# Ordering pieces of work behind gathers, opening sums by their first product, and loading weights later, in a four-layer graph network

## The chip, the cores and the metric

The kernel runs on one core of a Trainium2 chip. Its engines run side by side, each through its own queue in order: TensorE (PE, matmuls, with its weight loads shown as PEld), VectorE (DVE), ScalarE (ACT), GpSimd (POOL), and SyncE (SP), which here only issues DMAs. The metric is the device time of one execution in microseconds (us); lower is better.

## The reference, cut to what matters

There are 16 batches of 1024 nodes with 128 features, each with its own 1024 x 1024 adjacency. Four layers follow each other, and each adds its result to `x`:

```python
h = relu(layernorm(x)); x = x + layer0(h, adj, W0, b0)   # neighbours' mean, two weights
h = relu(layernorm(x)); x = x + layer1(h, adj, W1, b1)   # neighbours' mean, one weight
h = relu(layernorm(x)); x = x + layer2(h, adj, ...)      # two rounds of messages, below
h = relu(layernorm(x)); x = x + layer3(h, adj, W, a)     # attention over neighbours

# layer2, for l in (0, 1):
a, b = x @ We1[l, :D], x @ We1[l, D:]
scores = sigmoid(relu(a[:, :, None] + b[:, None] + be1[l]) @ We2[l] + be2[l])
messages = (adj * scores) @ x
x = layernorm(x + relu([x, messages] @ Wu1[l] + bu1[l]) @ Wu2[l] + bu2[l]) * gamma[l] + beta[l]

# layer3
e = leaky(Wh1 + Wh2.T) * (adj + I), masked; softmax; @ Wh; elu
```

About 1.6% of the adjacency is not zero, and layer 2 needs scores only there.

## The kernel before

Layer 2 is done edge by edge. The adjacency is cut into 128 x 128 blocks, called buckets; up to four buckets form one of nine `GROUPS`. For every bucket `build` makes four 0/1 matrices (`on`, `onT`, `om`, `omT`) that choose the two end nodes of each edge. A piece `pn` (PE, L829, in the helper `turned`) transposes `on`, and ACT evicts it to `onT` (L869). A piece `pq` (PE, L873) follows, and DVE makes `omT` of it (L876). A piece `pm` (L829 again) transposes that, and ACT evicts it to `om` (L884). The three pieces share the one PSUM bank "a".

A `round` (two for each batch) walks over the nine groups. For each bucket `gather` (L1015) multiplies the `part` tiles by `on` and `om`, four matmuls into a bank `pre`; ACT and DVE evict it into the two halves of `hid` (L1031, L1032). `dots` (L1048) multiplies `hid` into `sc`; `ends` (L1069) makes `srow`; `scores` transposes it (`pt`) and multiplies it onto `onT` and `omT` (`val`, L1106); `scatter` (L1131) makes blocks of scores in a bank `p`; DVE multiplies them by the adjacency (`upd`, L1139); and `messages` (L1148) adds their products with `xf` to the sums `msg`, one bank for each half of the nodes (`acc0`, `acc1`). Layer 3 sums its products (L507) in banks `hp`, over three stretches of nodes. Before such a sum begins, `zero` (L562, L563) writes zeros into the whole bank with a matmul of a zero matrix, and all products of the sum then add to it (`start=False`).

Each normalization runs through `spread`: `bn_stats` on DVE (L231), small DVE operations (L234 to L239), a power on POOL (L242), and then either DVE's L249 and eight ACT operations (L251) in `normal`, or the DVE operations from L363 on and four subtracts (L365) with `gamma` and `beta` (L370, L371) in `update`. The transposes that follow a norm are at L259 (`tp`); those of the updated nodes at L1181; the adjacency's at L754 (`tn`).

Three lanes are woven together by `weave`: `main` (the rounds of batch b), `last` (the second update and layer 3 of batch b - 1) and `first` (layers 0 and 1, the last norm and the buckets of batch b + 1). Each lane yields a price; `weave` always continues the lane whose sum of prices, divided by the lane's length (`MAIN_US` 184, `LAST_US` 70, `FIRST_US` 115), is least. From the program so written a scheduler sets each engine's final order. `tc.issue_after(ins)` keeps what is written inside it behind the instruction `ins` in an engine's order. Batch 0's `first` lane runs alone at the start (`run`), after the weights' DMAs, which are issued on ACT's queue (L103 to L138); between its first yield and the rest stands `scaled` (L607), which rescales weights through a chain of small PE, DVE and ACT steps.

Of the kernel before, what the change touches and what calls it, by code (L numbers as in the profile page):

```python
# [9 lines left out]
F32 = mybir.dt.float32  # L10
F16 = mybir.dt.float16
FP8 = mybir.dt.float8e4
I32 = mybir.dt.int32
AF = mybir.ActivationFunctionType
# [26 lines left out]


MAIN_US = 184.0
FIRST_US = 115.0
LAST_US = 70.0


# [4 lines left out]
def tile_four_gnn_layers(  # L52
# [22 lines left out]
    nc = tc.nc  # L75
    B, N, D = x.shape
    P = 128
    T = N // P
    HALF = 512
    NH = N // HALF  # L80
# [32 lines left out]
    for l in range(L):  # L113
        nc.scalar.dma_start(we1_sb[:, l], we1[l].rearrange("(h d) e -> d h e", h=2))
    b1_bc = const.tile([P, D], F32, name="b1_bc")
    nc.scalar.dma_start(b1_bc, b1[None, :].broadcast_to([P, D]))
    be2_bc = const.tile([P, L], F32, name="be2_bc")
    nc.scalar.dma_start(be2_bc, be2.rearrange("l o -> o l").broadcast_to([P, L]))
    wu1_sb = const.tile([P, L, 2, KB * P], F32, name="wu1_sb")
    wu2_sb = const.tile([P, L, KB, D], F32, name="wu2_sb")  # L120
    for l in range(L):
        nc.scalar.dma_start(wu1_sb[:, l], wu1[l].rearrange("(h d) k -> d h k", h=2))
        nc.scalar.dma_start(wu2_sb[:, l], wu2[l].rearrange("(k p) d -> p k d", p=P))
    bu1_sb = const.tile([P, L, KB], F32, name="bu1_sb")
    bu2_sb = const.tile([P, L], F32, name="bu2_sb")
    with nc.allow_non_contiguous_dma(reason="small columns of weights, once"):
        nc.scalar.dma_start(bu2_sb, bu2.rearrange("l d -> d l"))
        for l in range(L):
            nc.scalar.dma_start(bu1_sb[:, l], bu1[l].rearrange("(k p) -> p k", p=P))
    rows = {}  # L130
    for name, v in (("gamma", gamma), ("beta", beta)):
        rows[name] = const.tile([P, L, D], F32, name=f"{name}_bc")
        for l in range(L):
            nc.scalar.dma_start(rows[name][:, l], v[l : l + 1, :].broadcast_to([P, D]))
    w3_sb = const.tile([P, D], F32, name="w3_sb")
    nc.scalar.dma_start(w3_sb, w3)
    a3_sb = const.tile([P, 2], F32, name="a3_sb")
    nc.scalar.dma_start(a3_sb, a3.rearrange("(h d) o -> d (h o)", h=2))  # L138

    half_neg = const.tile([P, T], F32, name="half_neg")  # L140
    nc.vector.memset(half_neg, -0.5)
# [42 lines left out]

    def over_t(v, n=T):
        return v[:, None, :].to_broadcast([P, n, D])

    class Layers:

# [273 lines left out]
    class Lane(Layers):  # L463
# [2 lines left out]

        fine = None

        def layer3(self, xt, strip, zero, name):

            yield from self.pre_ln(xt, f"3_{name}")
            wh = self.wide(f"wh_{name}")
            nc.vector.memset(wh[:, :, D : D + 1], 1.0)
            for sl, ps in self.by_node(self.hT, w3_sb, f"wh_{name}"):
                nc.scalar.activation(wh[:, sl, :D], ps, AF.Copy)
                yield 1
            wh2, wh1 = self.score_terms(self.hT, 1, name)
            yield 2  # L480

            o = self.scratch(f"o3_{name}")
            rsum = self.small([P, 2, T], "rsum", f"rsum_{name}")
            for lo, hi in L3_ROWS:
                n = hi - lo
                sums = self.one(f"hp_{name}_{lo}")[:, : n * (D + 1)]
                zero(sums)
                sums = sums.rearrange("p (t d) -> p t d", d=D + 1)
                for k in range(0, T, 2):
                    at = strip(k, lo, hi)  # L490
                    e = flat(self.scratch(f"e_{name}_{lo}_{k}"))[:, : 2 * n * P]
                    e = e.rearrange("p (k n) -> p k n", k=2)
                    for i in range(2):
                        if lo <= k + i < hi:
                            own = at[:, i, (k + i - lo) * P : (k + i + 1 - lo) * P]
                            nc.vector.tensor_add(own, own, ident)
                        nc.vector.scalar_tensor_tensor(
                            e[:, i], wh1[:, lo * P : hi * P], wh2[:, k + i : k + i + 1], at[:, i],
                            op0=OP.add, op1=OP.mult,
                        )  # L500
                    nc.vector.scalar_tensor_tensor(e, e, L3_ALPHA, e, op0=OP.mult, op1=OP.max)
                    nc.scalar.activation(e, e, AF.Exp)
                    nc.vector.scalar_tensor_tensor(e, at, 0.0, e, op0=OP.is_gt, op1=OP.mult)  # L503
                    yield 0.4 * n
                    for i in range(2):
                        for t in range(n):
                            nc.tensor.matmul(  # L507
                                sums[:, t], e[:, i, t * P : (t + 1) * P], wh[:, k + i, : D + 1],
                                start=False, stop=True, skip_group_check=True,
                            )  # L510
                        yield 0.4 * n
                nc.vector.tensor_copy(rsum[:, 0, lo:hi], sums[:, :, D])
                nc.vector.reciprocal(rsum[:, 1, lo:hi], rsum[:, 0, lo:hi])
                for t in range(n):
                    nc.scalar.activation(
                        o[:, lo + t], sums[:, t, :D], AF.Copy, scale=rsum[:, 1, lo + t : lo + t + 1]
                    )
            self.sums_seen(rsum, name)
            self.layer3_end(xt, o, name)
# [10 lines left out]
    class Edges:  # L530
        def __init__(self, stack):
# [16 lines left out]
                Lane(self.work, "m", N_SCRATCH["m"], self.psum, [(f"acc{h}", 1)]) for h in range(NH)  # L548
            ]
            self.own, self.rows_of, self.n_rows = own, {}, 0  # L550
            self.constants()

        def bank(self, tag, name):
# [1 line left out]

        def acc(self, h, name):

            ps = self.psum.tile([P, HALF], F32, tag=f"acc{h}", name=name)
            self.zero(ps)
            return ps  # L560

        def zero(self, ps):  # L562
            nc.tensor.matmul(ps, self.zero16, self.iota2[:, : ps.shape[1]], start=True, stop=True)  # L563

        def constants(self):
            con = self.con
            self.eye16 = con.tile([P, P], F16, name="eye16")
            nc.vector.tensor_copy(self.eye16, ident)
            self.zero16 = con.tile([P, P], F16, name="zero16")
            nc.vector.memset(self.zero16, 0.0)  # L570
            self.ones16 = con.tile([P, 1], F16, name="ones16")
            nc.vector.memset(self.ones16, 1.0)
            self.iota2 = con.tile([P, HALF], F16, name="iota2")
# [154 lines left out]
        def first(self, b):  # L728
# [44 lines left out]
                xt, lambda t: self.load("a", self.columns(s.adjT, t), f"l1_{b}_{t}"), rdeg, name  # L773
            )
            s.xf = self.work.tile([P, T, D], F32, tag="xf0", name=f"xf0_{b}", bufs=1)
            yield from lane.pre_ln(xt, f"2_{name}", dst=s.xf)
            s.xT = self.kept(lane.hT, "xT", f"xT0_{b}")
            s.x = self.kept(xt, "x", f"xk_{b}")
            yield from self.build(s, has, name)

# [44 lines left out]
        def turned(self, hot, ck, name):  # L825

            ps = self.a.one(name)
            for k in range(ck):
                nc.tensor.matmul(  # L829
                    ps[:, k * P : (k + 1) * P], hot[:, k * P : (k + 1) * P], self.eye16,  # L830
                    start=True, stop=True,
                )
            return ps

        def build(self, s, has, name):

# [4 lines left out]
            for g, grp in enumerate(GROUPS):  # L841
# [13 lines left out]
                for i, (t, u) in enumerate(grp):  # L855
# [13 lines left out]
                    nc.scalar.activation(onT, pn[:, : ck * P], AF.Copy, saturate=False)  # L869
                    yield 0.35  # L870
                    pq = self.a.one(f"pq_{nm}").rearrange("p (k m) -> p k m", m=P)
                    for k in range(ck):
                        nc.tensor.matmul(  # L873
                            pq[:, k], on[:, k * P : (k + 1) * P], rank[:, i], start=True, stop=True
                        )
                    nc.vector.tensor_tensor(  # L876
                        omT.rearrange("p (k m) -> p k m", m=P), pq[:, :ck],
                        self.odd[t == u][:, :, None].to_broadcast([P, ck, P]),
# [84 lines left out]
        class Group:  # L963
# [41 lines left out]
            def gather(self, i):  # L1005
# [4 lines left out]
                for d in range(self.nd):  # L1010
                    pre = path.m.one(f"pre_{self.name}_{i}_{d}")

                    for v, node, hot in ((d, t, on), (1 - d, u, om)):
                        for k in range(2):
                            nc.tensor.matmul(  # L1015
                                pre[:, :c], path.parts[node // Q][:, k, node % Q, v], hot[:, :c],
                                start=(hot is on and k == 0),
                                stop=(hot is om and k == 1),
                            )
                    if not self.diag:  # L1020
                        hid = path.work.tile(
                            [P, 2, C_OFF], F16, tag="hid", name=f"hid_{self.name}_{i}_{d}", bufs=N_HID
# [122 lines left out]
            def messages(self, d, upd):  # L1145
                def message(mb, up, lo, hi):
                    h = lo // Q
                    nc.tensor.matmul(  # L1148
                        self.msg[h][:, (lo - h * Q) * P : (hi - h * Q) * P],
                        self.xf[mb // Q][:, mb % Q], up,  # L1150
                        start=False, stop=True, skip_group_check=True,
                    )

                if d:
# [63 lines left out]
        def last(self, s, b):  # L1218
# [19 lines left out]
                yield from lane.update(L - 1, s.xf[h], xT, msgT, dst, f"{b}_{L - 1}_{h}")  # L1238
            xt = self.back(self.work.tile([P, T, D], F32, tag="x", name=f"xb_{b}"), s.x)
            nc.vector.tensor_add(xt, xt, new)  # L1240
            yield from lane.layer3(xt, strip, self.zero, f"{b}")
            nc.sync.dma_start(out[b].rearrange("(t p) d -> p t d", p=P), xt)

        def run(self):
# [2 lines left out]
            self.alone(self.a, "amcam")  # L1247
            first = self.first(0)
            next(first)
            self.scaled()  # L1250
            for us in first:
                if us is None:
                    break

            self.alone(self.a, "")
            self.a.banks = [self.own["c"], self.own["a"]]
# [197 lines left out]
```

## Time and profile before

| | |
|---|---|
| median of 3 runs | 5316.95 us (5308.2 to 5318.65) |
| profiled execution | 5325.15 us, span 5323.4 us |
| mean granted TensorE clock | 0.983 |
| PE, DVE, ACT, POOL busy | 93%, 79%, 57%, 4% |
| start, before the first gather | 0 to 134.7 us |
| a batch, in the middle | some 322 to 325 us |
| DMA, mean over the span | 104 GB/s |

A busy share is the part of the span in which the engine had an instruction under way. Matmuls overlap, so the time of one in the profile is longer than the distance from its start to that of the next. "a <- b" with a wait means that instruction a had nothing ahead of it on its engine and waited until b had ended. The granted clock is the share of full speed that TensorE's throttle allowed. The three runs shown are not the profiled execution, which took 8.2 us more than their median.

### The profile page before, as it was taken

What the parts mean: (1) busy time and instruction counts of PE and PEld (TensorE: products, weight loads), DVE (VectorE), ACT (ScalarE), POOL (GpSimd) and SP (SyncE); (2) the same over time, 40 slices, a digit from 0 to 9 for tenths busy, and PEclk for the clock granted to TensorE, in tenths of its full rate; (3) what the DMA queues carried; (4) which work ended last, traced back from release to release, by engine and by line L of the source; (5) the groups of instructions that cost most, each with busy time, mean ns of one, the idle gap of its engine ahead of it and who ended that gap; (6) DMA issues with size and microseconds to landing.
All of it is one profiled execution on the core that took longest, in us unless ns stands there. A gap on an engine that the chain in (4) does not pass through costs nothing.

```text
span 5323.4 us, 112270 instructions
## 1 busy us (share of the span) xinstructions
PE 4977.0 (93%) x45109; PEld 3739.4 (70%) x45109; DVE 4216.4 (79%) x9543; ACT 3044.9 (57%) x6790; POOL 189.3 (4%) x137
## 2 busy tenths in 40 slices
PE   6999999999999999999999999999999999999986
PEld 5766777777777777777777777777767777777664
DVE  4776787877879778797887978878797887978876
ACT  5556564655646556475564756656465564755543
POOL 0000000000000000000000000000000000000000
PEclk8999999999999999999999999999999999999998
DMA  6242425243252433424334242432524334243121
GB/s 185 64 143 88 123 62 150 83 127 108 75 147 74 134 94 89 141 73 125 96 107 130 62 138 88 121 115 72 154 71 136 97 89 142 74 126 93 57 63 48
DMA packets 740130, 554.47 MB, mean 104 GB/s; under 512 B 32273, under 2 KB 686353, under 8 KB 739601
## 3 DMA queue, kind: packets, MB, share of 16 engines
q1 hardware_dynamic: 734496, 545.58, 34.4%
q8 instruction: 356, 5.83, 0.5%
q10 hardware_dynamic: 5104, 1.65, 0.1%
q14 instruction: 174, 1.42, 0.1%
HBM read 446.44 MB, written 100.66 MB: 103 GB/s over the span
## 4 chain that ended last, share of the span: by engine, by line
PE 55%; DVE 22%; ACT 12%; DMA 5%; issue 3%; POOL 2%; SPq 0%; ACTq 0%; POOLq 0%; DVEq 0%
PE pre L1015 14%; PE p L1131 7%; DVE val L1106 7%; PE nb L289 6%; PE msg L1148 5%; PE bb L297 3%; PE sc L1048 3%; DVE hid L1032 3%; DMA at<-in_adj_dram 3%; PE h L343 3%; PE hp L507 3%; ACT hid L1031 2%; PE pq L873 2%; PE pn L829 2%; DMA a<-adjT 2%
## 5 line engine op out<-in xcount | busy, mean ns | idle before, releaser
L1031 ACT ACTIVATE hid<-pre 128x320 f16<-128x320 f32 (+1 forms) x2048 | 915.6, 455 | 666.8 <-PE pre L1015 603.0
L1032 DVE SCALAR_TENSOR_TENSOR hid<-pre,hid 128x320 f16<-128x320 f32 (+1 forms) x2048 | 1006.8, 505 | 240.6 <-ACT hid L1031 227.0
L1015 PEld LDWEIGHTS <-part 128*128 128x128 f16 x8192 | 746.0, 98 | 404.8 <-issue 196.6
L1015 PE MATMUL pre<-on,part 128*128 128x320 fp8e4 (+1 forms) x4096 | 985.2, 310 | 42.7 <-DVE hid L1032 32.5
L1015 PE MATMUL pre<-om,part 128*128 128x320 fp8e4 (+1 forms) x4096 | 962.9, 309 | 0.0
L1148 PE MATMUL msg<-upd,xf 128*128 128x128 f32 (+3 forms) x3008 | 595.3, 320 | 0.3 <-DVE upd L1139 0.3
L1106 DVE TENSOR_TENSOR val<-onT,u 128x768 f32<-128x768 fp8e4 (+1 forms) x576 | 561.1, 1010 | 3.1
L1131 PE MATMUL p<-val,omT 128*128 128x128 f16 x6528 | 507.3, 219 | 23.4 <-DVE val L1106 13.4
L1131 PEld LDWEIGHTS <-omT 128*128 128x128 fp8e4 x6528 | 423.0, 96 | 89.6 <-issue 62.3
L884 ACT ACTIVATE om<-pm 128x320 fp8e4<-128x320 f32 (+1 forms) x576 | 269.8, 468 | 292.0 <-PE pm L829 289.3
L1148 PEld LDWEIGHTS msg<-upd,xf 128*128 128x128 f32 x3008 | 410.3, 192 | 15.7 <-DVE upd L1139 1.6
L1106 DVE TENSOR_TENSOR val<-omT,u 128x768 f32<-128x768 fp8e4 x448 | 410.7, 950 | 0.0
L1139 DVE SCALAR_TENSOR_TENSOR upd<-p,adj 128x512 f32<-128x512 f32 x512 | 348.9, 681 | 74.9 <-PE p L1131 69.8
L1131 PE MATMUL p<-val,onT 128*128 128x128 f16 x4480 | 375.2, 219 | 2.4 <-DVE upd L1139 2.4
L869 ACT ACTIVATE onT<-pn 128x384 fp8e4<-128x384 f32 (+1 forms) x576 | 297.9, 517 | 120.9 <-PE pn L829 97.3
L507 PE MATMUL hp<-wh,e 128*128 128x129 f32 x2048 | 330.0, 283 | 14.3 <-DVE e L503 14.0
L1069 ACT ACTIVATE srow<-sc,be_s,down 128x128 f32<-128x128 f32 (+2 forms) x512 | 256.2, 541 | 142.6 <-PE sc L1048 140.2
L1131 PEld LDWEIGHTS <-onT 128*128 128x128 fp8e4 x4480 | 304.9, 97 | 46.7 <-issue 14.5
L507 PEld LDWEIGHTS hp<-wh,e 128*128 128x128 f32 x2048 | 282.5, 193 | 48.3 <-issue 19.7
L820 DVE TENSOR_SCALAR on<-far,wid 128x384 fp8e4<-128x384 f16 (+1 forms) x576 | 242.3, 427 | 67.2 <-PE pre L1015 59.5
L1048 PE MATMUL sc<-hid,slide 128*32 128x320 f16 (+1 forms) x4096 | 281.0, 317 | 14.6 <-DVE hid L1032 10.7
L816 ACT ACTIVATE far<-iota_off,mid 128x384 f16<-128x384 f16 x448 | 273.6, 629 | 7.8 <-DVE on L820 4.8
(217 smaller groups left out, 8118.5 us busy)
## 6 DMA issues: line engine op xcount, KB each, us to landing
at<-in_adj_dram SPq DMA_DIRECT2D x128, 512.0 KB, 3.9
ct<-in_adj_dram SPq DMA_DIRECT2D x128, 512.0 KB, 4.4
adjT<-tn SPq DMA_DIRECT2D x128, 512.0 KB, 5.2
l<-adjT SPq DMA_DIRECT2D x128, 512.0 KB, 4.3
adj<-adjT SPq DMA_DIRECT2D x256, 256.0 KB, 3.6
a<-adjT SPq DMA_DIRECT2D x128, 384.0 KB, 3.3
adj<-adjT SPq DMA_DIRECT2D x448, 64.0 KB, 2.3
adj<-adjT SPq DMA_DIRECT2D x192, 128.0 KB, 2.7
```

What stands on the lines that cost most here:

```text
L289: nc.tensor.matmul(ps, mat[:, k], z[:, k], start=(k == 0), stop=(k == T - 1))
L507: nc.tensor.matmul(sums[:, t], e[:, i, t * P : (t + 1) * P], wh[:, k + i, : D + 1], start=False, stop=True, skip_group_check=True,)
L816: nc.scalar.activation(far[:, : ck * P], self.iota[t == u][:, : ck * P], AF.Abs, bias=s.mid[:, i : i + 1])
L869: nc.scalar.activation(onT, pn[:, : ck * P], AF.Copy, saturate=False)
L1015: nc.tensor.matmul(pre[:, :c], path.parts[node // Q][:, k, node % Q, v], hot[:, :c], start=(hot is on and k == 0), stop=(hot is om and k = ...
L1031: nc.scalar.activation(hid[:, 0, :c], pre[:, :c], AF.Relu)
L1032: nc.vector.scalar_tensor_tensor(hid[:, 1, :c], pre[:, :c], 0.0, hid[:, 0, :c], op0=OP.max, op1=OP.subtract)
L1048: ins = nc.tensor.matmul(self.sc[g * G : (g + 1) * G, : self.c], self.path.slide[:, self.l, G - 1 - r : 2 * G - 1 - r], self.hid[self.done ...
L1106: nc.vector.tensor_tensor(pair[:, :, :ck], right, v.rearrange("p k i o -> p i k o").to_broadcast([P, 2, ck, P]), op=OP.mult,)
L1131: nc.tensor.matmul(self.ps[d][:, i], left[:, k], halves[:, k, :, h], start=(k, h) == terms[0], stop=(k, h) == terms[-1],)
L1139: nc.vector.scalar_tensor_tensor(upd, self.ps[d], S_SCALE, self.adj[:, d * Q : (d + 1) * Q], op0=OP.add, op1=OP.mult,)
L1148: nc.tensor.matmul(self.msg[h][:, (lo - h * Q) * P : (hi - h * Q) * P], self.xf[mb // Q][:, mb % Q], up, start=False, stop=True, skip_grou ...
```

## The change

Four things are changed.

1. The matmuls that zero a bank are gone, and so is the zero matrix. A helper `add_to` gives the first product of each sum `start=True`, and keeps every other product of that sum behind it on PE.
2. `gather` records its last matmul in `path.gathered`. The pieces pn, pq and pm, and the last norm's transposes, are written inside `behind_rounds()`, that is, behind the latest gather recorded when they are written.
3. The last norm's transposes (`tp_2`) are written in `first` in two halves, with yields of 5, 4 and 1 in place of 2 and 2. `FIRST_US` is 121 in place of 115.
4. Seventeen of the weights' DMAs are moved into `load_rest`, which is called after the first yield of batch 0's `first` lane. `scaled()` is called when that lane has yielded nine more times, and no longer ahead of them.

```diff
-FIRST_US = 115.0
+FIRST_US = 121.0
...
+    def load_rest():
+
+        nc.scalar.dma_start(be2_bc, be2.rearrange("l o -> o l").broadcast_to([P, L]))
+        nc.scalar.dma_start(w3_sb, w3)
...
+            for name, v in (("gamma", gamma), ("beta", beta)):
+                nc.scalar.dma_start(rows[name][:, l], v[l : l + 1, :].broadcast_to([P, D]))
...
+    def add_to(opened, dst, left, right):
+
+
+        with ExitStack() as behind:
+            if opened is not None:
+                behind.enter_context(tc.issue_after(opened))
+            ins = nc.tensor.matmul(
+                dst, left, right, start=opened is None, stop=True, skip_group_check=True
+            )
+        return ins.ins if opened is None else opened
...
                 sums = self.one(f"hp_{name}_{lo}")[:, : n * (D + 1)]
-                zero(sums)
                 sums = sums.rearrange("p (t d) -> p t d", d=D + 1)
+                opened = None
...
-                            nc.tensor.matmul(
-                                sums[:, t], e[:, i, t * P : (t + 1) * P], wh[:, k + i, : D + 1],
-                                start=False, stop=True, skip_group_check=True,
+                            opened = add_to(
+                                opened, sums[:, t], e[:, i, t * P : (t + 1) * P], wh[:, k + i, : D + 1]
                             )
...
         def acc(self, h, name):
 
-            ps = self.psum.tile([P, HALF], F32, tag=f"acc{h}", name=name)
-            self.zero(ps)
-            return ps
-
-        def zero(self, ps):
-            nc.tensor.matmul(ps, self.zero16, self.iota2[:, : ps.shape[1]], start=True, stop=True)
+            self.opened[h] = None
+            return self.psum.tile([P, HALF], F32, tag=f"acc{h}", name=name)
...
-            yield from lane.pre_ln(xt, f"2_{name}", dst=s.xf)
-            s.xT = self.kept(lane.hT, "xT", f"xT0_{b}")
+            lane.normal(xt, s.xf, AF.Relu, f"2_{name}")
+
+            turned = lane.scratch(f"hT_2_{name}")
+            for h in range(NH):
+                yield 5 - h
+                with self.behind_rounds():
+                    half = slice(h * Q, (h + 1) * Q)
+                    ps = lane.one(f"tp_2_{name}_{h}").rearrange("p (t d) -> p t d", d=P)
+                    for i in range(Q):
+                        nc.tensor.transpose(ps[:, i], s.xf[:, h * Q + i], ident)
+                nc.scalar.activation(turned[:, half], ps, AF.Copy)
+            yield 1
+            s.xT = self.kept(turned, "xT", f"xT0_{b}")
...
         def turned(self, hot, ck, name):
 
             ps = self.a.one(name)
-            for k in range(ck):
-                nc.tensor.matmul(
-                    ps[:, k * P : (k + 1) * P], hot[:, k * P : (k + 1) * P], self.eye16,
-                    start=True, stop=True,
-                )
+            with self.behind_rounds():
+                for k in range(ck):
+                    nc.tensor.matmul(
+                        ps[:, k * P : (k + 1) * P], hot[:, k * P : (k + 1) * P], self.eye16,
+                        start=True, stop=True,
+                    )
             return ps
+
+        def behind_rounds(self):
+
+            return tc.issue_after(self.gathered) if self.gathered is not None else ExitStack()
...
+                    path.gathered = ins.ins
...
             next(first)
-            self.scaled()
-            for us in first:
+            load_rest()
+            for n, us in enumerate(first):
                 if us is None:
                     break
+                if n == 8:
+                    self.scaled()
```

`pq` and `message` are changed in the same way as `turned` and layer 3's products. In the changed kernel the lines stand some 10 to 35 further down; L377 there is L365 here.

More of the change, by code (lines that the diff above doesn't have):

```diff
@@ L115, in tile_four_gnn_layers @@
     b1_bc = const.tile([P, D], F32, name="b1_bc")
-    nc.scalar.dma_start(b1_bc, b1[None, :].broadcast_to([P, D]))
     be2_bc = const.tile([P, L], F32, name="be2_bc")
-    nc.scalar.dma_start(be2_bc, be2.rearrange("l o -> o l").broadcast_to([P, L]))
     wu1_sb = const.tile([P, L, 2, KB * P], F32, name="wu1_sb")
     wu2_sb = const.tile([P, L, KB, D], F32, name="wu2_sb")
-    for l in range(L):
-        nc.scalar.dma_start(wu1_sb[:, l], wu1[l].rearrange("(h d) k -> d h k", h=2))
-        nc.scalar.dma_start(wu2_sb[:, l], wu2[l].rearrange("(k p) d -> p k d", p=P))
@@ L124, in tile_four_gnn_layers @@
     bu1_sb = const.tile([P, L, KB], F32, name="bu1_sb")
     bu2_sb = const.tile([P, L], F32, name="bu2_sb")
-    with nc.allow_non_contiguous_dma(reason="small columns of weights, once"):
-        nc.scalar.dma_start(bu2_sb, bu2.rearrange("l d -> d l"))
-        for l in range(L):
[L129 to L138, printed above, removed]
+    rows = {name: const.tile([P, L, D], F32, name=f"{name}_bc") for name in ("gamma", "beta")}
+    w3_sb = const.tile([P, D], F32, name="w3_sb")
+    a3_sb = const.tile([P, 2], F32, name="a3_sb")
+    def load_rest():
+        nc.scalar.dma_start(be2_bc, be2.rearrange("l o -> o l").broadcast_to([P, L]))
+        nc.scalar.dma_start(w3_sb, w3)
+        nc.scalar.dma_start(a3_sb, a3.rearrange("(h d) o -> d (h o)", h=2))
+        nc.scalar.dma_start(b1_bc, b1[None, :].broadcast_to([P, D]))
+        with nc.allow_non_contiguous_dma(reason="small columns of weights, once"):
+            nc.scalar.dma_start(bu2_sb, bu2.rearrange("l d -> d l"))
+            for l in range(L):
+                nc.scalar.dma_start(bu1_sb[:, l], bu1[l].rearrange("(k p) -> p k", p=P))
+        for l in range(L):
+            nc.scalar.dma_start(wu1_sb[:, l], wu1[l].rearrange("(h d) k -> d h k", h=2))
+            nc.scalar.dma_start(wu2_sb[:, l], wu2[l].rearrange("(k p) d -> p k d", p=P))
+            for name, v in (("gamma", gamma), ("beta", beta)):
+                nc.scalar.dma_start(rows[name][:, l], v[l : l + 1, :].broadcast_to([P, D]))
@@ L467, in tile_four_gnn_layers, with layer3 @@
         fine = None
-        def layer3(self, xt, strip, zero, name):
+        def layer3(self, xt, strip, name):
             yield from self.pre_ln(xt, f"3_{name}")
@@ L550, in __init__ @@
             self.own, self.rows_of, self.n_rows = own, {}, 0
+            self.opened = [None] * NH
+            self.gathered = None
             self.constants()
@@ L568, in constants @@
             nc.vector.tensor_copy(self.eye16, ident)
-            self.zero16 = con.tile([P, P], F16, name="zero16")
-            nc.vector.memset(self.zero16, 0.0)
             self.ones16 = con.tile([P, 1], F16, name="ones16")
@@ L871, in build @@
                     pq = self.a.one(f"pq_{nm}").rearrange("p (k m) -> p k m", m=P)
[L872 to L875, printed above, removed]
+                    with self.behind_rounds():
+                        for k in range(ck):
+                            nc.tensor.matmul(
+                                pq[:, k], on[:, k * P : (k + 1) * P], rank[:, i], start=True, stop=True
+                            )
                     nc.vector.tensor_tensor(
@@ L1014, in gather @@
                         for k in range(2):
-                            nc.tensor.matmul(
+                            ins = nc.tensor.matmul(
                                 pre[:, :c], path.parts[node // Q][:, k, node % Q, v], hot[:, :c],
@@ L1147, in message @@
                     h = lo // Q
-                    nc.tensor.matmul(
-                        self.msg[h][:, (lo - h * Q) * P : (hi - h * Q) * P],
+                    self.path.opened[h] = add_to(
+                        self.path.opened[h], self.msg[h][:, (lo - h * Q) * P : (hi - h * Q) * P],
                         self.xf[mb // Q][:, mb % Q], up,
-                        start=False, stop=True, skip_group_check=True,
                     )
@@ L1240, in last @@
             nc.vector.tensor_add(xt, xt, new)
-            yield from lane.layer3(xt, strip, self.zero, f"{b}")
+            yield from lane.layer3(xt, strip, f"{b}")
             nc.sync.dma_start(out[b].rearrange("(t p) d -> p t d", p=P), xt)
```

## Prediction

> **What bounds it.** The page's first part comes first.
>
> ```profile
> PE 4977.0 (93%) x45109; PEld 3739.4 (70%) x45109; DVE 4216.4 (79%) x9543; ACT 3044.9 (57%) x6790; POOL 189.3 (4%) x137
> ```
>
> PE, the matmul engine, is busy 93% of the span, DVE 79%. An average hides stages, so I cut the span into stretches (busy time of each engine): the first 135 us hold 82 us of PE work, 470 to 5140 us hold 4450 in 4670 (95%), the last 183 hold 130. Inside the batches PE is the bound. What can be won there is PE work removed, or the 220 us in which PE waits, at most. So the list of PE's waits for 135 to 5140 us is next (waiting line, releaser, total us, times, longest):
>
> ```profile
> PE tp L259 <- ACT xf L251: 33.5, 14, 2.4
> PE pm L829 <- DVE omT L876: 28.6, 48, 1.0
> PE pre L1015 <- DVE hid L1032: 24.7, 43, 1.5
> ...
> PE pn L829 <- ACT om L884: 16.0, 44, 0.5
> PE tp L1181 <- DVE xf L371: 15.1, 14, 1.1
> ...
> PE pq L873 <- ACT onT L869: 11.1, 30, 0.6
> ```
>
> The diff touches the first wait (the last norm's transposes, once a batch) and three of the others (the bucket pieces pn, pq, pm: 55.7 us together). The timeline of PE around one such transpose shows its price:
>
> ```profile
> 1929.99 0.43 PE L1015 MATMUL pre<-om,part 128*128 128x320 fp8e4 x2
> 1932.82 0.33 PE L259 MATMUL tp<-ident,xf 128*128 128x128 f32 x1 [2.40 <-ACT xf L251]
> ...
> 1935.00 0.74 PE L1015 MATMUL pre<-om,part 128*128 128x320 fp8e4 x2
> ```
>
> 2.40 us of nothing, and afterwards a pair of gather matmuls takes 0.74 us where it took 0.43. The stretches table for 1930 to 1938 us gives a granted clock of 0.80 against 1.00 in the 8 us before: some 1.7 us more. A site costs 4 to 5 us a batch.
>
> **The skill.** Three places bear on it. "TensorE: Matmul & The Clock Gate", Part 1, says that the array falls to half clock after an idle activity window of about 3.4 us and that the windows run freely; the 0.43 to 0.74 us and the 0.80 above agree in kind, though here a 2.40 us gap sufficed. "PSUM — Partial Sum Buffer", The four PSUM rules, says that a product with the first flag clears the written bits of what it covers, and that later products overwrite where the bit is clear and add where it is set: the zeroing product can go if one product of each sum opens it and comes first. No line of this trace shows that. "DMA: Bandwidth & Descriptors", Issuing engines are not separate DMA queues, says that DMAs of all issuing engines share 16 DMA engines and another issuer saves only issue time: moving 17 weight DMAs later on ACT's queue can win what ACT spends issuing, no transfer time.
>
> **The change, part by part.** The sum is against the profiled execution, 5325.15 us (span 5323.4, 1.75 outside), which is 8.2 above the median shown, 5316.95.
>
> *Zeroing products.* The rows of L563:
>
> ```profile
> L563 PE MATMUL msg<-iota,zero x64: 377/379/634, 12.1 to 5139.9; 128*128 128x512 f16 x64
> L563 PE MATMUL hp<-iota,zero x48: 273/327/328, 581.4 to 5279.5; 128*128 128x387 f16 x32, 128*128 128x258 f16 x16
> ```
>
> Matmuls are pipelined, so I price by starts: at 2076.85 us a 512-wide one starts and its successor at 2077.06 (216 ns from the unrounded records); the 387-wide ones take 164 ns, the 258-wide 110. 64 x 216 + 32 x 164 + 16 x 110 ns = 20.8 us. PE is nearly always the bound there, so I take **-19**; both ends: -21 (all on the path) and 0 (were each beside a wait). The order it adds holds one sum's products behind its opener, on the same engine; that opener needs the same upd or e as before, so I price it at nothing; should an opener stand late, the others queue behind it, up to 1 us for each of 32 halves, and I keep +10 in the range.
>
> *Weights and scaled().* ACT's queue issues 22 DMAs, and only then its first norm runs, though DVE's part was ready at 12.43:
>
> ```profile
> 18.12 0.45 ACTq L138 DMA_DIRECT2D a_sb<-in_L_gnn_a_dram  x1
> 18.59 1.28 ACT L251 ACT_TABLE_LOAD   x1 [18.59 <-DMA gamma_bc<-in_L_gnn_gamma_dram]
> ```
>
> In the changed program's order 19 DMAs still stand ahead of that norm, so only some three issues of about 0.4 to 0.7 us go: **-2** (0 to -6). The moved scaled() lets the first adjacency transposes go ahead of its chain. That chain (matmuls at 30.21, 31.79, 33.79, 35.63 us, each behind a DVE or ACT step) holds them until
>
> ```profile
> 36.49 1.33 PE L754 MATMUL tn<-ident,at 128*128 128x128 f32 x5
> ```
>
> In the new order they follow bb matmuls of about 27 us: 9 us earlier. What follows, 40 to 75 us, is bound by DMA (share 0.98), and 25 to 40 has a DMA share of 0.03 because no row buffer comes free; so the stage slides forward, **-9**. scaled()'s chain now lies in that stage, whose PE is 26 of 35 us busy; its in-order waits may delay strips: **+3** (0 to +9). Sum -8 (0 to -14).
>
> *Bucket pieces behind the latest gather.* Comparing the two programs' orders of 1728 pn/pq/pm groups against the gathers: 775 stand the same, 728 later, 225 earlier; mean +0.4 gather. The waits are short (0.3 to 0.6 us each), about one gather of four matmuls (4 x 135 ns = 0.54 us). If the 42% that move later lose their wait, 55.7 x 0.42 = -23; the 13% that move earlier get one, +6: **-17** (-35 to +10: the shared bank "a" may merely pass the wait from one piece to the next).
>
> *The last norm's transposes.* In the old order no PE work lies between POOL's power and the first tp_2; in the new one 4.4 us do, so the 2.4 us wait goes, and with it up to 4.8 x 14 batches = 67, of which I keep at most -40. What is late next: in the new order DVE's queue, after the update norm's subtract (after L377), its gamma product and then a hid, waits for POOL's power first. PE's next sc needs that hid, and stands 3.6 us of PE work behind the tx transposes. The chain between is tx, xf 0.68, hid 0.64, bn_stats 0.9, on 0.48, small ones 0.7, POOL 1.3, four subtracts 1.1, gamma 0.68, hid 0.64: about 8 us. So a wait of 4 to 5 us stands where 2.4 went. POOL's price in the old trace:
>
> ```profile
> 1930.40 1.64 POOL L242 TENSOR_TENSOR st<-st,half_neg 128x8 f32<-128x8 f32 x1 [31.77 <-DVE st L239]
> 1933.84 1.32 POOL L242 TENSOR_TENSOR st_y<-st_y,half_neg 128x4 f32<-128x4 f32 x1 [1.80 <-DVE st_y L363]
> ```
>
> I take **0** (-40 to +17, both by 14 batches).
>
> *POOL's other powers.* DVE waits for POOL (L249) 60.3 us in 46 times already. In four sites of a batch the new order has less DVE work between the small operations and POOL's consumer: st_0 2.55 us before, 0 after; st_y of layer 1, half 1, 4.1 and 0; two others lose their PE cover behind a hid. Each leaves up to 1.2 to 1.7 us on PE; one site gains 0.5. Net +3.9 x 14 = 55 if nothing gives it back. DVE is 81% busy there, and PE has other lanes, so I halve it: **+27** (0 to 55).
>
> Sum: -19 - 8 - 17 + 0 + 27 = -17, 5308 against the profiled execution, **5300** against the median.
>
> **Rivals.** *Slower: the DVE queue behind POOL.* DVE runs in order, and a hid that stands behind a consumer of POOL's power stops PE's sc, with the half clock after it. At full price: 55 + 17 - 19 - 8, pieces at half, -8 = +37, **5354**. It decides once these waits exceed some 44/14 = 3.1 us a batch (19 + 8 + 17 to be used up). For it: the orders themselves and the 60.3 us row; against it: DVE has slack of 19%, so a wait may be made up before PE arrives. *No change: given back.* PE loses the zeros and gets as much waiting at pre: -27 - 17 + 44, **5317**. For it: the row of pre behind hid, which grows whenever PE runs ahead of ACT and DVE (a gather's two evictions take 455 and 505 ns). *Much faster.* The 2.4 us gap and its half clock go and no new wait comes: 40 more than the forecast, **5260**. For it: 4.4 us of new cover; against it, the chain of 8 us. *That the orders do not bind* (the pieces are as ready as before, and the tie moves nothing on the chip) leaves zeros and start, less what the halves cost: near the forecast.
>
> **The numbers.** Forecast 0.35, much faster 0.12, no change 0.17, slower 0.36. About 0.2%, 10.6 us, is what a measurement of this kernel can tell from no change. The forecast lies 17 below the median, just beyond that, and its own range is 5275 to 5325. Faster by over 0.2%: nine tenths of the forecast's 0.35, 0.12, and 0.02 of no change, 0.46; within it, the rest of these two, less 0.01, 0.17; slower, 0.36 + 0.01 = 0.37. The 8-in-10 range has to hold both signs: 5240 (much faster with the pieces at their best) to 5362 (slower with the pieces' gain lost).
>
> **What would show it.** Right: L563 is gone; PE's busy time falls by some 20 us; the wait of tp behind xf falls from 33.5 to below 10; the pieces' three rows fall from 55.7 to about 40; the first tn stands near 27 us and the first gather some 8 us before 134.7; DVE's waits for POOL grow by 30 or more and PE's waits at sc and pre with them. Wrong: sc and pre wait no more than before (then it is much faster), or the clock of the 8 us after a tp_2 stays at 0.80 with a PE wait over 4 us (then slower); pieces waiting as long as before would strike the -17.

## The result, and the profile after

The changed kernel takes 5325.23 us in the median of four runs, against 5317.11 for the kernel before: a ratio of 1.0020 with a 95% interval of 1.0003 to 1.0038. It is slower by about as much as a measurement can tell from no change (8 us by the medians, 10.6 by the ratio). The forecast was 5300; the sign was wrong.

The first part of the page after:

```profile
PE 4951.2 (93%) x44997; PEld 3734.8 (70%) x44997; DVE 4222.8 (79%) x9542; ACT 3048.3 (57%) x6790; POOL 175.6 (3%) x137
```

112 matmuls are gone and PE is busy 25.8 us less, about what was forecast (20.8). The span is not shorter (5324.4 against 5323.4 us), so PE waits more. Its waits from 135 to 5140 us, in the columns used before (line, releaser, total us, times, longest):

```profile
PE sc L1073 <- DVE hid L1057: 74.5, 45, 3.4
PE pre L1039 <- DVE hid L1057: 31.8, 67, 1.6
PE nb L301 <- ACT tn L762: 24.8, 31, 1.8
PE pq L897 <- ACT onT L892: 21.1, 30, 1.4
PE pm L848 <- DVE omT L900: 19.1, 49, 0.9
...
PE pn L848 <- ACT rank L876: 9.6, 14, 0.7
...
PE pn L848 <- ACT om L908: 5.0, 14, 0.5
...
PE tp L1205 <- DVE xf L383: 1.5, 2, 0.9
```

The wait of the last norm's transposes behind xf (33.5 us) has left the list, and that of the updated nodes' transposes fell from 15.1 to 1.5. In their place stands sc behind hid, 74.5 us where it was 7.5. Before, from the same stretch:

```profile
PE tn L754 <- ACT tn L755: 17.9, 20, 2.3
...
PE p L1131 <- DVE val L1106: 12.8, 45, 0.8
...
PE sc L1048 <- DVE hid L1032: 7.5, 11, 1.4
```

The pieces' rows did not shrink: 21.1, 19.1 and 5.0, with 9.6 behind the rank, are 54.8 us, against 55.7. One site of sc's wait in the timeline, PE first (start, busy us, engine, line, then the wait in brackets):

```profile
1917.28 0.43 PE L1039 MATMUL pre<-om,part 128*128 128x320 fp8e4 x2
1921.11 0.99 PE L1073 MATMUL sc<-hid,slide 128*32 128x480 f16 x8 [3.39 <-DVE hid L1057]
```

and DVE in the same microseconds:

```profile
1918.64 1.11 DVE L377 TENSOR_SCALAR xf<-xf,st_y 128x128 f32<-128x128 f32 x4 [0.90 <-POOL st_y L254]
1919.79 0.69 DVE L382 TENSOR_TENSOR xf<-xf,gamma_bc 128x512 f32<-128x512 f32 x1
1920.40 0.65 DVE L1057 SCALAR_TENSOR_TENSOR hid<-pre,hid 128x480 f16<-128x480 f32 x1
```

This is the chain of the prediction: the hid that sc needs stands on DVE behind the update norm's four subtracts and the product with gamma, and these wait for POOL. DVE's waits for POOL's other powers grew too, as foreseen (before, then after, 135 to 5140 us):

```profile
DVE st L249 <- POOL st L242: 60.3, 46, 1.8
DVE st L261 <- POOL st L254: 97.0, 58, 1.8
```

Still these waits will turn out not to be what made the kernel slower.

The start went as forecast:

```profile
15.73 1.28 ACT L263 ACT_TABLE_LOAD   x1 [15.73 <-DMA wu_sb<-in_L_gnn_Wu_dram]
25.91 0.60 PE L761 MATMUL tn<-ident,at 128*128 128x128 f32 x4
```

ACT's first norm is ready to start 2.9 us earlier (18.59 before), the first adjacency transpose stands 10.6 us earlier (36.49), and the first gather at 125.7 us, 9.0 earlier.

### The profile page after: what moved, and what is told of

Its sections match the earlier page's. It is cut to its first block, busy times and chain, and to the rows that moved or that the text cites. A ratio compares the mean times of both kernels' runs of the same rounds, so it can differ in the third digit from the quotient of the medians.

```text
span 5324.4 us, 112185 instructions
## 1 busy us (share of the span) xinstructions
PE 4951.2 (93%) x44997; PEld 3734.8 (70%) x44997; DVE 4222.8 (79%) x9542; ACT 3048.3 (57%) x6790; POOL 175.6 (3%) x137
## 4 chain that ended last, share of the span: by engine, by line
PE 56%; DVE 21%; ACT 10%; DMA 8%; issue 3%; POOL 2%; ACTq 0%; DVEq 0%; SPq 0%; POOLq 0%
PE pre L1039 14%; DVE val L1131 6%; PE p L1156 6%; PE nb L301 6%; DMA at<-in_adj_dram 5%; PE msg L195 4%; PE sc L1073 4%; DVE hid L1057 4%; PE bb L309 4%; PE h L355 3%; PE hp L195 3%; DMA a<-adjT 2%; PE pn L848 2%; PE pq L897 2%; ACT h L263 2%
## 5 line engine op out<-in xcount | busy, mean ns | idle before, releaser
L301 PE MATMUL nb<-z,ct 128*128 128x128 f32 x2048 | 265.2, 281 | 27.1 <-ACT tn L762 25.1
L900 DVE TENSOR_TENSOR omT<-pq,odd_off 128x384 fp8e4<-128x384 f32 x448 | 248.0, 554 | 52.2 <-PE pq L897 49.7
```

Of the source, the lines that this page charges most:

```text
L301: nc.tensor.matmul(ps, mat[:, k], z[:, k], start=(k == 0), stop=(k == T - 1))
```

## The experiments

Differences in us below are the ratio less one, times the median of the kernel before as measured beside that run. The runs were taken on three chips, where the kernel before took 5309.07 us (the four parts), 5318.36 (pad320 to start_halves_hid) and 5321.52 (the rest): across these groups compare the differences, not the times. For the stretch between the first gather of batch 2 and that of batch 15 (13 batches, no start and no end in it) I split the time of a profiled execution into three: PE idle; the extra of the half clock, which is half of PE's busy time inside the stretches that the records give at half clock; and the rest, the matmul work at full clock. Half is taken because, in the timeline of before, the distance from one gather pair to the next goes from 0.27 to 0.53 us in such a stretch.

**The four parts, each alone on the kernel before.** Their edits are the four parts of the diff above; nothing is left out.

*z_sums*, the zeroing products away and the sums opened by their first products:

> The kernel before with the zeroing products alone taken away (each sum opened by its first product, the others behind it); nothing else is changed. Theory A (the changed kernel lost at one new wait, and every other part gave what it promised): PE's busy time falls by 20.8 us and the time by 15 to 20 us. Theory B (PE has slack in its waits, so that work taken from it comes back as waiting for DVE and ACT): busy time falls by 20.8 us, PE's waits for hid grow by about as much, and the time falls by less than 8 us.

Measured: 5326.37 us, ratio 1.0029 (1.0020 to 1.0039), 15.4 us **slower**. Both theories fail. PE is busy 11.7 us less than in the profile before, and waits more:

```profile
PE p L1142 <- DVE val L1117: 45.8, 47, 1.5
PE tn L760 <- ACT tn L761: 30.5, 27, 2.0
```

p behind val was 12.8 us and tn behind tn 17.9. A wait of p longer than any in the kernel before (0.8 us), in the timeline of PE:

```profile
1844.77 0.43 PE L1025 MATMUL pre<-om,part 128*128 128x320 fp8e4 x2
1846.65 0.74 PE L1142 MATMUL p<-val,omT 128*128 128x128 f16 x10 [1.45 <-DVE val L1117]
```

The scatter stands in PE's order ahead of its operand. Over the 13 batches, against z_pieces below (whose matmuls have the order of before), idle goes from 184.8 to 203.1 us, the half clock's extra from 31.7 to 32.4 and the work at full clock from 3972.5 to 3961.6: 19 us of zeroing are gone, the other matmuls cost 8 us more, and the waits 18 us more. I compared the programs' orders: without the zeroing products the scheduler puts 6529 of some 43800 matmuls out of the order of before. The theory that this suggests, and that the next runs test: the products' work was small, and their absence made another order.

*z_start*, weights and scaled() alone:

> The kernel before with the start alone changed: 17 weight DMAs behind the first layer's first yield, and the rescaling of weights nine yields later. Theory A: the first gather stands near 125.7 us as in the changed kernel (134.7 before), the rest keeps its pace, and the time falls by 8 to 10 us. Theory B: the first gather is earlier, but the end moves by less than 4 us, since a later stage takes the gain back.

Measured: 5299.16 us, ratio 0.9979 (0.9969 to 0.9989), 11.1 us faster; the first gather stands at 124.8 us, 9.9 earlier. Theory A. (The diff moves fifteen of the weights' DMAs, not seventeen, and in the changed kernel's trace three of them come behind the first norm.)

*z_pieces*, the pieces behind the latest gather alone:

> The kernel before with the bucket pieces alone written behind the latest gather. The step on record was -17 us, from three rows of waits that would fall from 55.7 us to about 40. Theory A, after the changed kernel's rows (45.2 us, and 9.6 us more behind the rank): the waits only change places inside the pieces, and the time moves by less than 5 us either way. Theory B: the step on record holds, 12 to 20 us less.

Measured: 5310.68 us, ratio 0.9997 (0.9988 to 1.0005). The order says why: not one of the 43800 or so matmuls stands elsewhere. The tie binds nothing, so this run is also a second profile of the kernel before. The two profiles differ over the 13 batches by 6.7 us of idle, 4.6 of half clock and 1.8 of work, and differences of that size say nothing. In the changed kernel, leaving the tie out moves 63 matmuls; that was not run. But all_but_sums, below, is start_halves with the tie: 19.2 us faster than before against 26.1, with intervals that overlap, so nothing was gained by it there either.

*z_halves*, the last norm's transposes in halves with their yields and 121 us:

> The kernel before with the last norm's transposes alone changed: in two halves behind a gather, yields of 5, 4 and 1, and a first lane of 121. Theory A: this part alone makes the new wait of sc behind hid (7.5 us before, about 70 expected, of 3.4 us in each of 14 batches with the hid on DVE behind POOL's power), takes away the 33.5 us of tp behind xf and most of the 15.1 us at the transposes of updated nodes, and slows the program by 20 to 40 us. Theory B: the new wait comes from the parts together, and this part alone is within 8 us of before or faster.

Measured: 5298.95 us, ratio 0.9976 (0.9967 to 0.9985), 12.7 us **faster**, with the new wait in full:

```profile
PE sc L1077 <- DVE hid L1061: 76.3, 59, 3.4
PE pre L1043 <- DVE hid L1061: 37.7, 84, 1.4
```

Theory A had the wait right and the sign wrong, theory B the reverse. Over the 13 batches, against z_pieces: idle 184.8 to 197.8 us, half-clock extra 31.7 to 25.2, work at full clock 3972.5 to 3956.7. The same matmuls cost 15.8 us less PE time in this order, and that is well beyond the 1.8 between two profiles of one order; the half clock's 6.5 is hardly beyond its 4.6. Grouped by tile (each matmul's start to the next one's start), sc has the largest part, 12.9: 190.5 to 177.6 us. Other tiles gain or lose up to some 10 us each and nearly cancel. What sc depends on is seen in the timeline: a group of eight that runs through, and one with a piece between (z_sums, then changed_again):

```profile
1788.78 0.46 PE L1059 MATMUL sc<-hid,slide 128*32 128x320 f16 x8
1789.17 0.31 PE L1025 MATMUL pre<-on,part 128*128 128x320 fp8e4 x1
```

```profile
1963.53 0.45 PE L1073 MATMUL sc<-hid,slide 128*32 128x320 f16 x6
1964.00 0.33 PE L848 MATMUL pn<-eye,on 128*128 128x128 f16 x3
1964.26 0.31 PE L1073 MATMUL sc<-hid,slide 128*32 128x320 f16 x2
1964.50 0.45 PE L1039 MATMUL pre<-on,part 128*128 128x320 fp8e4 x2
```

The whole group holds PE for 0.39 us; the split one for 0.47 and 0.24, besides the piece. Medians over a trace at full clock: 388 ns for eight, 246 for two and 382 for six, so a split costs sc 0.24 us. The piece pays as well: three pn products hold PE for 258 ns between two stretches of sc and for 165 between gathers. sc's 512 groups in all 16 batches stand in 625 stretches in the kernel before, 678 in z_sums, 561 in z_halves: 53 x 0.24 = 13 us more and 64 x 0.24 = 15 us less (52 of the 64, 12.5 us, in the 13 batches). That the splits cause the difference is worked out from these, not tried by itself.

**Work or order.** The opened sums of z_sums are replaced by a narrow zeroing product, and all products of its sum are tied behind it, with `start=False`; the cut shows the kernel before against the product's new form:

```diff
-            nc.tensor.matmul(ps, self.zero16, self.iota2[:, : ps.shape[1]], start=True, stop=True)
+            n = min(320, ps.shape[1])   # 384, 64 in other runs
+            return nc.tensor.matmul(ps[:, :n], self.zero16, self.iota2[:, :n], start=True, stop=True).ins
```

*pad320:*

> The kernel before with its zeroing products kept, but 320 columns wide at most (they clear the bank's marks all the same, and every product of the sum is held behind them). Some 15 of their 20.8 us are still paid, but the scheduler's order of matmuls is near that of the kernel without them (2125 of 43802 matmuls out of that order, 5165 out of the order of before). Theory A (the order that the scheduler makes is what costs, not the work): slower than before by 10 to 35 us, with p waiting for val some 30 us more than before. Theory B (taking the work away is what costs): within 5 us of before or faster.

Measured: 5328.50 us, ratio 1.0020 (1.0012 to 1.0027), 10.6 us slower; p waits for val 19 us more than before, where 30 were expected:

```profile
PE p L1149 <- DVE val L1124: 32.0, 47, 1.4
```

*pad384:*

> As the run of 320 columns, with 384 columns at most. Some 3.5 us of the zeroing are saved, and 549 of 43802 matmuls stand out of the order of before (6453 out of that of the kernel without zeroing). Theory A: 0 to 7 us faster than before, waits of p for val as before (12.8 us). Theory B: it falls between before and the kernel without zeroing, 0 to 6 us slower.

Measured: 5315.95 us, ratio 0.9995 (0.9987 to 1.0003), 2.7 us faster, which can't be told from no change, and

```profile
PE p L1149 <- DVE val L1124: 11.9, 43, 0.8
```

Theory A in both, though pad384 by itself hardly parts the theories. The pair does: between these two kernels the zeroing differs by under 3 us, and the time by 13, five times as much and the other way from what taking work away should do. The time goes with the order, not with the work.

**Do the parts add up?** *start_halves*, with the zeroing products kept and the pieces untied:

> The later weights and the transposes in halves together; the zeroing products kept and the pieces not tied. If the parts add up: 11 + 13 = 24 us faster than before (18 to 28), ahead of the changed kernel by some 30. Rival (they meet in the same waits): 8 to 14 us faster.

Measured: 5292.33 us, ratio 0.9951 (0.9938 to 0.9965), 26.1 us faster: they add up.

*start_halves_hid:*

```diff
             nc.vector.tensor_scalar(mean, mean, 0.5, None, op0=OP.mult)
-            for t in range(Q):
+            yield 0
+            yield 0
+            with tc.issue_after(Layers.late_hid) if self.lane == "m" else ExitStack():
+                for t in range(Q):
...
-                    nc.vector.scalar_tensor_tensor(
+                    late = nc.vector.scalar_tensor_tensor(
                         hid[:, 1, :c], pre[:, :c], 0.0, hid[:, 0, :c], op0=OP.max, op1=OP.subtract
                     )
+                    Layers.late_hid = late.ins
```

> As start_halves, with two more steps between the update norm's small operations and its four subtracts, which are held on DVE behind the latest hid: PE's sc no longer waits for a hid behind POOL's power. Theory A (that wait, 76 us in the run of the halves alone, is PE's own loss): sc's waits fall below 30 us and the time by 25 to 50 us against start_halves. Theory B (PE is paced by DVE or by the throttle's windows there, so the wait returns elsewhere): the sum of PE's waits falls by less than 20 us and the time by less than 12.

Measured: 5294.25 us, ratio 0.9956 (0.9942 to 0.9969), 23.4 us faster than before: no gain on start_halves. Theory B. The wait did shrink (sc behind hid was 76.8 us in start_halves),

```profile
PE sc L1082 <- DVE hid L1065: 50.6, 41, 1.8
PE pre L1047 <- DVE hid L1065: 37.9, 71, 1.6
PE pq L905 <- ACT onT L901: 25.0, 42, 1.1
PE pn L857 <- ACT om L916: 23.0, 56, 0.5
```

and no stretch of half clock is left in the 13 batches (24.9 us of extra in start_halves); the mean granted clock of its five runs is 0.988 to 0.990, against 0.984 to 0.985. But the order moved here too (4747 matmuls): pq and pn wait 15 us more, idle goes from 201.5 to 205.7, and work at full clock from 3957.4 to 3973.3. So the run does not show what the wait alone is worth.

**The sums inside the changed kernel.** *all_but_sums* is the changed kernel with its zeroing products back; *changed_again* is the changed kernel on the same chip.

> The changed kernel with the zeroing products back and nothing else undone; on PE its order differs from start_halves in 88 of 43802 matmuls. Theory A (the opened sums cost through the order that the scheduler makes without the zeroing, in the changed kernel too): 20 to 30 us faster than before, as start_halves (26), so that the opened sums cost the changed kernel 25 to 40 us. Theory B (the parts meet elsewhere, start_halves was fast for want of the pieces' tie): within 10 us of before.

> The changed kernel once more, on the same chip as all_but_sums. Both theories: 2 to 20 us slower than before, as it was; groups of eight sc matmuls split 130 times (49 in start_halves), about 0.24 us each.

Measured: all_but_sums 5300.28 us, ratio 0.9964 (0.9950 to 0.9978), 19.2 us faster than before, a little short of the range of theory A, with an interval (11.7 to 26.6) that leaves out B's; changed_again 5329.06, ratio 1.0014 (1.0007 to 1.0021), 7.5 us slower, with the 130 splits that were expected. The opened sums cost the changed kernel 27 us. In the stretches table for the 13 batches each line has from and to, the length, busy us of PE, PEld, DVE, ACT and POOL with their counts, the granted clock, and DMA's share and GB/s; all_but_sums comes first, changed_again second:

```profile
775.20:4965.80 4190.60, 3984.12 (x36635) 3019.42 (x36633) 3411.71 (x7699) 2479.05 (x5504) 138.91 (x103) 0.99 0.36 107
```

```profile
766.90:4979.80 4212.90, 3986.18 (x36538) 3013.92 (x36536) 3418.01 (x7696) 2463.49 (x5503) 139.03 (x103) 0.99 0.36 106
```

Ninety-odd products fewer, 18.0 us of zeroing by start to start, and yet PE is busy 2.1 us longer and idle 226.7 against 206.5 us. By tile, sc rose from 177.8 to 198.8 us (642 stretches against 562 in all 16 batches, 80 x 0.24 = 19 us) and msg by 13.

**The fastest.** *start_halves_384* and *start_halves_64* are start_halves with narrow zeroing products.

> start_halves with zeroing products of 384 columns at most (order of start_halves but for 71 matmuls), 3.5 us of PE work less. Theory A: 0 to 6 us faster than start_halves was, 26 to 32 faster than before.

Measured: 5294.46 us, ratio 0.9952 (0.9938 to 0.9965), 25.5 us faster than before, just short of the range; it cannot be told from start_halves.

> start_halves with zeroing products of 64 columns: 17 us of PE work less than start_halves, but an order of its own (5473 matmuls moved; the sc groups are split 26 times more, 6 us). Theory A (order decides, and split groups are part of it): anywhere from 12 us faster to 25 slower than start_halves, and the difference is found in the splits and in the waits of p for val, not in the zeroing. Theory B (order is indifferent, work counts): 10 to 17 us faster than start_halves.

Measured: 5283.47 us, ratio 0.9933 (0.9919 to 0.9946), 35.7 us faster: the best of all, ahead of both kernels. Its slowest run (5287.28) is faster than the fastest of start_halves_384 (5291.12), measured beside it. Against start_halves the work at full clock falls by 20.1 us in the 13 batches (3937.3), 14 of it zeroing; idle rises by 2.0 and the half-clock extra by 8.1, so that about half is kept. p waits for val here as well (29.0 us where it was 7.9), but other waits went (pq behind onT 4.0 after 17.5, pm behind omT 3.0 after 11.5). The 9.6 us gained on start_halves are just short of B's range and inside A's, which was wide; the run does not decide between them.

## Why the prediction was wrong, step by step

- **Zeroing products, -19.** This is the step that failed. The product's price was about right (18.0 us in 13 batches, start to start; 20.8 in 16 would be 16.9), and the ties on the opener move nothing: with the zeroing products kept at full width, not one matmul stands elsewhere for them. But the step priced the removal as if everything else stayed where it was. What the runs show in its place is a new order of PE's queue, with 6529 of its matmuls elsewhere: on the kernel before the removal gave +15, inside the changed kernel +27, and pad320 and pad384 show that it is the order that makes the time. I had counted how the orders differ, and charged the differences to the pieces and to the halves; I never asked which part made them.
- **Start, -8.** Right: -11 alone.
- **Pieces, -17.** Wrong: nothing. The tie does not bind, and the 42% of pieces that I saw standing later owed it to other parts. The rival that the orders do not bind was true of this part.
- **The last norm's transposes, 0, and POOL's other powers, +27.** Mechanism right, sum wrong. The wait of sc came as worked out, 67 us more in all against 47 of tp waits that went, a net of 20. (By the prediction's own chain, 4 to 5 us in place of 2.4 in 14 batches, it would have been 22 to 36; the bound of 17, for the time, does not follow from it as written.) pre behind hid rose by 7 us in the changed kernel and by 13 in z_halves, and DVE's waits for POOL (st) from 60.3 to 97.0 and 89.2. The two steps together were +27, and this part alone measured -13. What I left out is that the same order made PE's work 15.8 us cheaper in 13 batches and the half clock 6.5, the latter hardly more than two profiles of one order differ by.
- **The sum.** The rival "no change" has the nearest time, 5317, and the nearest picture, PE's saved work returned as waits, but it named pre behind hid as the row that would grow, and that grew by only 7. The rival "slower" has the sign and foresaw the waits of sc, but not the cause: the part that makes these waits is 12.7 us faster by itself, and the loss comes from the removal that this rival counted as 19 us won. That the sign fits it is luck. The parts alone add to 15.4 - 11.1 - 1.6 - 12.7 = -10; the changed kernel has +8 because the sums cost 27 in it and not 15, and because the other three together gave 19 (all_but_sums) and not 25, which is within the intervals.
- **Not settled:** how the cost of the order divides between split sc groups and late operands, since every edit that moved one moved the other; and which piece of the third part (the halves, their tie, the yields, the 121) makes its better order, since they were only tried together.

## What to carry to other kernels

Where a scheduler sets the order, an instruction that is removed is also a cost removed from its plan: compare the orders with that one edit alone, before pricing it at its duration. A tie is checked in the same way: if it moves no instruction, it is worth nothing. When an order has moved, look at waits and also at what the same instructions cost in the new order, such as groups that ran overlapped and are now split; and try an edit that removes work at several sizes. Here the narrower product that kept the old order (384 columns) gained too little to measure, and the two that moved it went either way: 10.6 us lost at 320 columns, some 10 won at 64 in another context.

## What the runs showed of the hardware

A group of eight 320-column matmuls that each write 32 of the 128 rows takes 388 ns uninterrupted, but 246 + 382 ns when other matmuls stand between its first two and its last six: 0.24 us more. Three 128-column pn products that stand in between hold PE for 258 ns, against 165 between gathers. Freeing 13 batches of every half-clock stretch (start_halves_hid, against 24.9 us of extra in start_halves) did not shorten them measurably, while idle and work grew by 20 us; half clock, idle and work traded places there, so none of them may be booked as a gain by itself in this kernel. A matmul with `start=True` over 64 columns (start_halves_64) opened sums over banks of up to 512, and a first product of 129 columns one of 387 (layer 3 in the changed kernel): every other product added with `start=False`, and the sums came out right.
